# Moving the subtraction of the cumulative sums, 256 instructions, from VectorE to GpSimd in a Mamba-2 and ternary-FFN kernel

## The chip, the cores and the metric

The kernel runs on one core of a Trainium2 chip. A core has a matrix engine (TensorE, PE in the profile), three engines for elementwise work (VectorE or DVE, ScalarE or ACT, GpSimd or POOL) and a queue that issues the DMAs (SyncE, SP). Each engine takes its instructions in the order in which the program lists them and waits on semaphores for the others. The metric is device time in microseconds, lower is better.

## The reference

4096 tokens (2 sequences of 2048, width 512) go through a Mamba-2 layer, a residual sum and layer norm, a gated feed-forward layer with ternary weights, and a second residual sum and layer norm, all in float32. What matters here is the scan of the Mamba layer:

```python
dA = jnp.moveaxis(dtr * A, -1, -2)
xdt = xr * dtr[..., None]
Lmat = _segsum_exp(dA)      # exp(cum[s] - cum[z]) for z <= s, else 0
Y_diag = jnp.einsum('bcshn,bczhn,bchsz,bczhp->bcshp', Ch, Bh, Lmat, xdt)
cum = jnp.cumsum(dA, axis=-1)
decay_states = jnp.exp(cum[..., -1:] - cum)
states = jnp.einsum('bczhn,bchz,bczhp->bchpn', Bh, decay_states, xdt)
...
Y_off = jnp.einsum('bcshn,bchpn,bchs->bcshp', Ch, prev_states, jnp.exp(cum))
y = (Y_diag + Y_off).reshape(b, l, h, p)
...
hidden = silu(x @ wu.T) * (x @ wg.T);  out = hidden @ wd.T
```

There are 8 heads of 128 channels and a state of 64. The reference's chunks have 64 tokens; the kernel uses chunks of 128, which gives the same sums. For each chunk and head it needs the differences cum[s] - cum[z] for all 128x128 pairs of tokens. Only those with z <= s count, and for these the difference is at most zero; the kernel limits the others to zero so that the exponential cannot overflow, and masks them later.

## The kernel before

**Tiling.** The tokens are taken in 16 groups of 256 (`TG`), each of two chunks of 128 (`NC`). `proj(g)` does the input projections of a group, `steps(g)` the step sizes and the cumulative sums, `exps(g)` the exponentials, and `scan(g, c)` the scan of a chunk with the output projection. After that the feed-forward layer runs in 8 blocks of 512 tokens (`pair`, `down`); each of its products is made of seven smaller ones in fp8 and fp16. The first 45 us of the profile are preparation, the groups lie at about 45 to 745 us, and the feed-forward layer fills the rest.

**The path of a group around the change.** `cmm` (line 860) is the matmul that makes the cumulative sums. VectorE copies them out of PSUM: `ct` (864), 16 rows of 128, and `cum` (865), one column for each chunk and head. SyncE writes `ct` to DRAM (867) and reads it back spread over all 128 partitions: `cr` (873), one tile of 128 partitions x 8 heads x 128 for each chunk, 512 KB, and `ec` (887), used for the part that comes from the state before. Then `seg` (878) subtracts from each 128x128 block of `cr` the column `cum` and limits the result to zero: 8 instructions for a chunk in two half-operations of four (`sg{c}{hf}`), 16 for a group, 256 in all. ScalarE takes the exponential of the whole tile in place: `xf` (896) for the first chunk, `xg` (897) for the second, and `xec` (899) for `ec`. These need another activation table than the SiLU work around them, so `xf` has been made to wait for the second chunk's `cr` and for both `ec` tiles too, to do all exponentials of a group in one visit to that table. In the scan `w` (919) takes one column of the exponential, `xw0` (934) weighs B with it for the matmul that makes the new state (`st`, 941), `m` (956, eight instructions) multiplies the tile by the step size and by B.C masked, `md` (958) adds the D term, and `yd` (963) multiplies the result with x. After that `yg` (965), the sum of squares `ssq` (970), `rs` (971), the power on GpSimd `pw` (972), `yh` (973), a DMA transpose `th` (974) and the output projection `o0` to `o2` (983) follow.

**The projections.** Each projection result in PSUM (`x0` to `x8`, line 779) goes through a convolution of four taps: the first on ScalarE (`t3`, 792), three on VectorE (794), then SiLU on ScalarE (`xs`, 798) and a transpose on PE (`xt`, 802), which ScalarE evicts (804). The gate columns (`z`, line 754) are evicted by ScalarE (768).

**GpSimd before.** Beside a few instructions at the start, GpSimd computes only powers of 128x1 columns: `pw` (972) in the scans, the same for the inputs (636) and in the layer norms (1206, 1254).

**What sets the order.** The program is recorded as a list of operations, each with an engine, an assumed cost and what it reads and writes. `Order.run` then makes the order of each engine: it walks through an assumed time, and of the operations that are ready for an engine takes the one with the smallest key. The keys are a table of numbers in the source (`KEYS`), one for each operation, which a search outside of the kernel has found; on the chip no key and no assumed cost is known, only the order that came out. Buffers are handed out in the same walk, so the order also decides which buffer an operation gets. The assumed cost of one `seg` instruction is 0.197 us on VectorE.

Of the kernel before, what the change touches and what calls it, by code (L numbers as in the profile page):

```python
# [23 lines left out]
NH = 8  # L24
# [17 lines left out]
140 139 245 183 268 349 233 268 348 194 134 321 296 448 210 232 291 190 119 151 181 177 348 247 218 261 115 305 164  # L42
156 191 164 299 171 402 237 384 367 385 734 917 930 182 172 214 387 415 409 155 325 203 200 94 160 411 337 214 337
306 163 337 337 398 327 152 395 396 161 424 399 370 532 576 542 630 514 661 622 639 762 564 135 134 239 197 239 175
264 316 219 65 355 279 384 295 420 283 449 508 614 674 694 896 928 938 689 786 668 873 896 964 889 1242 891 879 920
999 856 952 1038 862 772 996 138 22 76 34 102 42 112 114 329 138 130 112 99 188 298 84 176 176 107 -9 160 159 116
228 128 172 210 252 211 348 304 268 316 448 420 282 390 703 399 394 474 429 430 431 395 523 337 463 372 462 456 506
687 744 752 824 727 794 786 782 88 348 349 169 216 212 185 465 437 664 529 411 520 533 514 508 544 572 535 552 573
594 574 575 512 592 592 684 540 600 745 640 687 606 625 698 681 289 225 340 448 309 142 340 370 436 348 176 190 353
303 273 175 379 282 662 640 695 696 597 682 778 667 200 316 294 129 255 19 205 231 602 626 650 607 735 517 783 670  # L50
369 283 422 447 626 339 450 353 549 385 632 679 549 255 600 642 617 779 763 660 708 652 712 701 264 514 514 538 827
520 575 638 528 653 736 692 226 314 489 471 146 173 56 172 214 182 117 630 408 305 608 674 535 671 685 738 681 720
717 1085 685 717 932 870 877 900 873 849 862 891 839 950 947 1129 940 946 975 1019 997 898 913 1088 936 1171 1438
989 989 1139 1105 997 437 344 217 489 494 615 643 593 586 512 384 223 402 421 480 368 470 638 782 725 786 797 739
827 999 1068 421 391 426 397 406 450 807 777 511 453 602 559 538 638 675 710 1142 1095 1194 1098 1113 1034 1154 1228
940 1055 950 984 1020 1098 1229 1360 984 1048 1193 967 973 1187 1224 1086 531 551 671 557 576 776 937 1032 889 894
1312 1249 1199 1067 797 830 563 573 764 795 790 827 876 878 839 1007 748 903 912 1329 1056 1066 1158 1072 981 1141
998 1103 1170 1206 1444 1395 529 563 797 869 796 778 793 855 882 844 861 839 924 829 830 913 924 908 912 980 935 949
1046 1060 993 1059 1066 966 1272 193 389 496 575 873 572 615 680 629 1188 938 1028 916 1051 1133 1161 872 1133 1225
1078 1364 1222 1382 1412 1405 1415 1480 1388 1472 1405 1454 1474 1368 1476 1560 1475 1499 1564 1415 1338 1504 1438  # L60
1394 1526 1636 1374 1214 1537 1818 1314 767 595 684 789 809 880 893 748 1006 1054 796 718 816 838 802 984 1082 1249
979 789 988 1060 920 1363 1338 1294 701 655 707 599 719 875 1052 986 836 875 884 954 973 1184 1031 1013 1034 1078
1065 1107 1189 1229 1079 1122 1066 1215 1085 1215 857 1204 1355 1433 1172 1198 1018 1265 1347 1277 1356 1530 614 658
733 656 649 699 835 939 1324 1361 928 872 1286 1397 1030 1049 949 1047 1156 1374 1354 1024 1410 1321 1413 1070 1400
1305 1414 1269 1291 1285 1291 1295 1478 1156 1426 1215 1403 1303 1441 1446 1439 1769 1394 866 991 1300 1389 1379
1436 1406 1368 1637 1239 1522 1397 1289 1278 1546 1392 1528 1790 1537 1618 1612 1259 1635 1357 1711 1648 1599 1996
1848 1240 1288 1412 1359 1425 1235 1428 1557 1445 1443 1380 1334 1574 1479 1520 1614 1624 1640 1871 1749 1972 2068
1842 1771 1752 1797 1815 1863 1829 1704 1917 1920 1807 1989 1852 2037 1664 2336 1769 1954 1996 1986 1920 1827 1994
1818 1746 1933 1887 1822 869 1331 1482 1499 1511 1601 1522 1496 1478 1709 1313 1514 1516 1516 1491 1564 1435 1675
1495 1702 1559 1609 1538 1847 1635 1608 1536 1737 1709 1709 1623 1827 1750 1929 1552 1749 1700 1656 1692 1974 1869  # L70
1918 1759 1949 1877 1875 1983 1875 1701 1913 1402 1735 1613 1553 1580 1673 1541 1764 1317 1624 1590 1516 1496 1614
1510 1621 1455 1699 1581 1324 1524 1689 1665 1798 2011 1967 1689 1808 1909 1873 1660 1905 1251 1309 1632 1626 1716
1572 1437 1581 1772 1690 1692 1665 1740 1664 1697 1679 1789 1550 1792 1718 1811 1747 1919 2171 1754 1870 1861 2146
2078 1142 1229 1681 1732 1920 1867 1880 1546 2129 1933 1964 1802 1940 1784 1812 1705 1962 2095 2094 1878 1958 1936
2031 1906 1961 2109 2118 1986 2525 1816 1668 1775 1706 1694 1981 1786 1974 1838 2093 1857 1906 2115 1910 2020 1866
1984 2047 2155 1960 2107 1921 2179 2123 1998 2150 2055 2086 2121 2075 2026 2123 1953 2053 2077 1979 2079 2327 2178
2162 2282 2376 2291 2472 2482 2308 2258 2103 2339 2344 1886 1735 1754 1933 1963 1960 1829 1888 2162 2209 1782 2008
2008 2049 1977 2311 2168 2061 1973 2081 1936 1949 1795 2227 2141 2162 1805 1998 2012 1797 1874 2141 1970 2023 1830
1908 1695 1888 1973 2186 1990 1932 2122 2067 2181 2052 2123 1999 2130 2127 1685 2023 1776 1892 1799 1900 1884 2028
2122 2253 2334 2339 2329 2055 2330 2304 1960 2014 1954 1918 1998 2119 2112 1971 2099 1992 2257 2154 2144 2273 2191  # L80
2156 1483 1637 1927 2118 2183 2206 2115 2057 1942 2171 2120 2216 2359 2036 2147 2040 2086 2181 2341 2192 2259 2268
2310 2489 2266 2369 2526 2438 2489 1689 1833 2030 2182 2257 2240 2194 2247 2498 2251 2150 2213 2309 2141 2170 2164
2351 2370 2327 2539 2485 2355 2460 2421 2457 2462 2448 2606 2785 2328 2087 2227 2195 2202 2320 2285 2305 2421 2198
2239 2384 2272 2296 2412 2263 2332 2203 2645 2223 2450 2405 2616 2457 2539 2774 2490 2613 2502 2585 2673 2676 2732
2752 2541 2462 2657 2714 2693 2933 2749 2911 2908 2518 2768 2820 2995 2645 2771 2889 2355 2276 2340 2475 2361 2370
2531 2413 2605 2533 2411 2199 2395 2619 2460 2468 2543 2587 2264 2325 2494 2403 2293 2455 2375 2488 2610 2488 2604
2680 2552 2614 2716 3088 2659 2488 2624 2622 2570 2876 2729 2797 2398 2445 2620 2354 2452 2575 2626 2697 2374 2577
2420 2458 2490 2316 2674 2906 2869 2734 2332 2532 2477 2752 2583 2749 2664 2615 2632 2681 2642 2874 2764 2925 3149
3124 3048 3154 3124 3092 3076 2931 1999 2139 2305 2593 2611 2521 2384 2454 2587 2474 2539 2681 2547 2479 2616 2516
2465 2692 2555 2745 2690 2694 2678 2803 2696 2873 2817 2764 3052 2216 2399 2423 2687 2704 2561 2711 2688 2895 2630  # L90
2598 2527 2807 2618 2560 2590 2549 2890 2726 2957 3025 3119 2945 2875 2907 2947 2915 3215 3424 2205 2544 2494 2403
2242 2393 2370 2730 2358 2828 2878 2725 2800 2911 2557 2863 2467 2834 2956 2899 3018 2820 2684 2608 2702 2797 2723
2784 2875 2884 3020 2942 2983 2915 2994 2938 3056 3163 3100 3053 3057 3280 3118 3484 3444 3266 3320 3221 3341 3430
3163 3101 2969 3134 3139 3269 3211 3132 3262 3338 2760 2710 2599 2661 2539 2813 3129 3048 3083 3125 2898 2982 2836
3056 3043 3099 2978 3118 2762 2775 2693 3117 3110 3184 2756 2965 2546 2636 2733 3367 3087 3195 2698 2895 2586 2635
2631 3039 3099 3136 3164 3232 3074 3254 3142 3341 3190 3293 3103 3068 3288 3069 3062 3095 3132 3112 2518 2457 2752
2477 2558 2722 3017 2999 2682 3140 3249 3245 3217 3137 3071 3016 2785 2599 2669 2780 2747 3099 2615 3052 3037 2827
2860 3068 3101 2745 2769 3080 3044 3166 3125 3060 3222 3235 3300 3265 3337 3297 3324 3464 3418 2672 2432 3081 2834
2916 3185 3134 3233 3384 3161 3160 3284 3280 2867 3017 3196 3213 3407 3280 3289 3365 3338 3394 3319 3419 3437 3421
# [261 lines left out]
class Order:  # L361
# [48 lines left out]
    def keys(self):  # L410
        for o, k in zip(self.ops, KEYS.split(), strict=True):
            o.key = int(k) / 10
# [100 lines left out]
def mamba_ffn_kernel(  # L513
# [51 lines left out]
    with ExitStack() as ph:  # L565
# [266 lines left out]
        def steps(g):  # L832
# [36 lines left out]
            for c in range(NC):  # L869
# [5 lines left out]
                for hf in range(2):  # L875
                    def seg(c=c, cr=cr, hf=hf):
                        for h in range(hf * 4, hf * 4 + 4):
                            V.tensor_scalar(cr[:, h, :], cr[:, h, :], cum[:, c * NH + h:c * NH + h + 1], 0.0, ALU.subtract, ALU.min)  # L878
# [433 lines left out]
```

## Time and profile before

| | us |
|---|---|
| median of 3 runs (1355.98 to 1358.28) | 1356.5 |
| span of the profiled execution, first to last instruction | 1355.1 |
| PE busy | 1334.2 (98%) |
| VectorE busy | 1143.1 (84%) |
| ScalarE busy | 1041.0 (77%) |
| GpSimd busy | 80.4 (6%) |
| the 256 `seg` instructions on VectorE: busy, idle just before them | 54.0, 6.6 |

The median of the runs is 1.4 us above the span of the profiled execution, the fastest run 0.9 us. A matmul is busy in the profile from its start to the end of its way through the array, 0.27 us for one that follows the last after 0.11 us, so neighbours overlap and PE can be called busy over a short pause. GpSimd durations are rough.

### The profile page before, as it was taken

To read this page: it belongs to the slowest core of one execution; us is meant where nothing else is said; L and a number is where in the kernel's file an instruction comes from. 1 tells how busy PE (TensorE), PEld (TensorE's weight loads), DVE (VectorE), ACT (ScalarE), POOL (GpSimd) and SP (SyncE) were. 2 spreads that over 40 slices of the span, in tenths; PEclk is the share of its full clock that TensorE was granted. 3 is DMA by queue.
4 is the path that set the end of the run, shared out by engine and by line. 5 is a ranking of instruction groups with operands and counts; after the bars stand their busy time and mean duration, and the time that the engine had idled before them with its cause. 6 is when DMAs were issued, how large, how long until landed. Compare 5 with 4: busy or idle time off the path is not lost.

```text
span 1355.1 us, 28913 instructions
## 1 busy us (share of the span) xinstructions
PE 1334.2 (98%) x11024; PEld 1057.9 (78%) x11024; DVE 1143.1 (84%) x3070; ACT 1041.0 (77%) x1996; POOL 80.4 (6%) x127
## 2 busy tenths in 40 slices
PE   9999999999999999999999999999999999999997
PEld 7777667766776677777676788888888888888886
DVE  5988878878999889889888697987979797979985
ACT  8888777768788778787767695969778695959772
POOL 1000000000000010000000000101010100001000
PEclk9999999999999999999999999999999999999999
DMA  6445666534543553573439530413222231314101
GB/s 242 139 116 147 171 164 165 147 111 124 155 137 99 156 139 80 137 185 85 112 76 247 127 63 9 125 24 110 40 79 55 94 56 60 82 40 102 32 17 47
DMA packets 194811, 145.60 MB, mean 107 GB/s; under 512 B 140656, under 2 KB 151920, under 8 KB 194672
## 3 DMA queue, kind: packets, MB, share of 16 engines
q1 hardware_dynamic: 194672, 143.75, 40.7%
q8 instruction: 86, 1.41, 0.4%
q14 instruction: 53, 0.43, 0.1%
HBM read 89.84 MB, written 22.41 MB: 83 GB/s over the span
## 4 chain that ended last, share of the span: by engine, by line
PE 66%; DVE 17%; ACT 10%; DMA 4%; issue 2%; POOL 0%; SPq 0%; POOLq 0%; ACTq 0%; DVEq 0%
PE sd L1096 9%; PE mm L779 9%; PE po L983 8%; PE mm L754 8%; PE po L1148 5%; PE sd L1148 4%; PE mm L1096 3%; PE po L1096 3%; PE sd L963 3%; DVE acc L794 3%; PE ms L1148 2%; DVE cr L956 2%; PE ms L1096 2%; PE mm L1148 2%; PE tr L802 2%
## 5 line engine op out<-in xcount | busy, mean ns | idle before, releaser
L1096 PEld LDWEIGHTS <-wx 128*128 128x128 fp8e4 x2048 | 200.2, 98 | 27.3 <-issue 2.9
L794 DVE SCALAR_TENSOR_TENSOR acc<-mm,cwu,acc 128x256 f32<-128x256 f32 x405 | 189.3, 479 | 21.6 <-ACT acc L792 19.2
L779 PEld LDWEIGHTS <-wx 128*128 128x128 f16 x1620 | 155.6, 97 | 33.2 <-issue 1.1
L1096 PEld LDWEIGHTS <-wz 128*128 128x128 fp8e4 x1536 | 150.2, 98 | 22.8 <-issue 4.6
L779 PE MATMUL mm<-uh,wx 128*128 128x260 f16 x1080 | 142.8, 274 | 0.7 <-DVE acc L794 0.5
L754 PE MATMUL mm<-wz,uh 128*128 128x344 f16 x720 | 119.9, 309 | 2.5 <-DVE acc L794 1.4
L983 PE MATMUL po<-wo,th 128*128 128x512 f16 x512 | 121.0, 379 | 0.3 <-ACT js L986 0.3
L792 ACT ACTIVATE acc<-mm,cst,cwu 128x256 f32<-128x256 f32 x135 | 74.8, 556 | 33.3 <-PE mm L779 31.8
L754 PEld LDWEIGHTS <-uh 128*128 128x128 f16 x720 | 68.5, 98 | 37.5 <-issue 4.4
L983 PEld LDWEIGHTS <-th 128*128 128x128 f16 x512 | 49.0, 98 | 49.5 <-issue 1.2
L779 PE MATMUL mm<-ul,wx 128*128 128x260 f16 x540 | 82.1, 273 | 0.0
L768 ACT ACTIVATE sz<-mm,szs 128x344 f32<-128x344 f32 (+1 forms) x90 | 48.4, 539 | 33.1 <-PE mm L754 28.4
L956 DVE SCALAR_TENSOR_TENSOR cr<-cr,dt,gm 128x128 f32<-128x128 f32 x256 | 72.1, 347 | 0.3
L798 ACT ACTIVATE xc<-acc 128x256 f32<-128x256 f32 x128 | 52.3, 412 | 25.5 <-DVE acc L794 25.1
L754 PE MATMUL mm<-wz,ul 128*128 128x344 f16 x360 | 67.2, 309 | 0.0
L963 PE MATMUL sd<-xt,cr 128*128 128x128 f32 x512 | 66.5, 277 | 0.1
L963 PEld LDWEIGHTS sd<-xt,cr 128*128 128x128 f32 x512 | 62.0, 192 | 3.1 <-issue 0.7
L983 PE MATMUL po<-wo,tl 128*128 128x512 f16 x256 | 60.5, 379 | 0.0
L878 DVE TENSOR_SCALAR cr<-cr,cum 128x128 f32<-128x128 f32 x256 | 54.0, 281 | 6.6 <-DMA cr<-cum_scratch 6.6
L804 ACT ACTIVATE xt<-tr 128x256 f32<-128x256 f32 x128 | 47.9, 374 | 11.7 <-PE tr L802 10.7
L1148 PEld LDWEIGHTS <-xt 128*128 128x128 f16 x512 | 50.1, 98 | 6.6 <-DVE xt L1131 0.9
L802 PE MATMUL tr<-ident,xc 128*128 128x128 f32 x256 | 50.2, 278 | 0.2
(356 smaller groups left out, 3275.1 us busy)
## 6 DMA issues: line engine op xcount, KB each, us to landing
cr<-cum_scratch SPq DMA_DIRECT2D x32, 512.0 KB, 5.6
ec<-cum_scratch SPq DMA_DIRECT2D x64, 128.0 KB, 5.5
fraw<-in_wupT_dram SPq DMA_DIRECT2D x32, 256.0 KB, 3.4
s_scratch<-js SPq DMA_DIRECT2D x32, 256.0 KB, 2.3
x<-s_scratch SPq DMA_DIRECT2D x32, 256.0 KB, 3.1
fraw<-in_wgateT_dram SPq DMA_DIRECT2D x32, 256.0 KB, 3.1
fraw<-in_wdownT_dram SPq DMA_DIRECT2D x32, 256.0 KB, 3.1
uraw<-in_uT_dram SPq DMA_DIRECT2D x15, 520.0 KB, 3.8
```

Of the source, the lines that this page charges most:

```text
L754: T.matmul(ps[:, :ZC], (uh, ul)[a][:, k, HL + c * P:HL + (c + 1) * P], wz4[b]()[:, j, k, :], start=(n == 0), stop=(n == 11))
L779: T.matmul(ps[:, :TW], wx4[a]()[:, j, k, :], (uh, ul)[b][:, k, :], start=(n == 0), stop=(n == 11))
L792: op(f"t{j}3", "S", act(TG, 2), lambda: S.activation(acc.ap, ps[:, HL:TW], AF.Identity, bias=cb[:, j:j + 1], scale=tap(3)), r=[ps, kc] + k ...
L794: op(f"t{j}{k}", "V", stt(TG), lambda k=k: V.scalar_tensor_tensor(acc.ap, ps[:, 1 + k:1 + k + TG], tap(k), acc.ap, ALU.mult, ALU.add), r=[ ...
L798: op(f"xs{j}", "S", silu(TG), lambda: S.activation(xc.ap, acc.ap, AF.Silu), r=[acc], w=[xc], table="silu")
L802: T.transpose(tr[:, c * P:(c + 1) * P], xc[:, c * P:(c + 1) * P], ident)
L878: V.tensor_scalar(cr[:, h, :], cr[:, h, :], cum[:, c * NH + h:c * NH + h + 1], 0.0, ALU.subtract, ALU.min)
L956: V.scalar_tensor_tensor(cr[:, h, :], cr[:, h, :], dt[:, c, h:h + 1], gm.ap, ALU.mult, ALU.mult)
L963: T.matmul(yp[hf][:, i * P:(i + 1) * P], cr[:, h, :], xt[:, c, h, :], start=is_first(g, c), stop=(is_first(g, c) or i == 3))
L983: T.matmul(po.ap, t[:, k, :], wo3[b]()[:, k, :], start=(q == 0 and k == 0), stop=(q == 2 and k == 7))
L1096: T.matmul(bank_[:, fi * TG:(fi + 1) * TG], wt[:, kt, f * P:(f + 1) * P], xT[i][:, a, :, kt, :], start=(first and fi == 0 and n == 0), sto ...
L1148: T.matmul(bank_[:, s_ * TG:(s_ + 1) * TG], X[k][j][:, a, e, s_ * P:(s_ + 1) * P], wt[:, k, :], start=(first and s_ == 0 and k == 0 and a ...
```

## The change

The subtraction with its limit at zero is issued on GpSimd instead of VectorE, with the same tiles and the same values; nothing else in the computation changes. The assumed cost in the planner becomes 0.3 us for each instruction. The table of keys is replaced as a whole, with numbers ten times finer, so that the order of every engine, the DMA queue's included, is a new one from the beginning to the end.

```diff
 KEYS = """
-140 139 245 183 268 349 233 268 348 194 134 321 296 448 210 232 291 190 119 151 181 177 348 247 218 261 115 305 164
...
-13374 13478 13544 13584 13460 13428 13216 13539 13325 13239 13477 13532 13619 13275 13367 13487 13497 13434
...
+138470 110551 -118248 107267 -122697 103243 -6098 122038 32505 -74957 106546
 """
...
         for o, k in zip(self.ops, KEYS.split(), strict=True):
-            o.key = int(k) / 10
+            o.key = int(k) / 100
...
                     def seg(c=c, cr=cr, hf=hf):
                         for h in range(hf * 4, hf * 4 + 4):
-                            V.tensor_scalar(cr[:, h, :], cr[:, h, :], cum[:, c * NH + h:c * NH + h + 1], 0.0, ALU.subtract, ALU.min)
-                    op(f"sg{c}{hf}", "V", 4 * 0.197, seg, r=[cum], w=[(cr, hf)])
+                            G.tensor_scalar(cr[:, h, :], cr[:, h, :], cum[:, c * NH + h:c * NH + h + 1], 0.0, ALU.subtract, ALU.min)
+                    op(f"sg{c}{hf}", "G", 4 * 0.3, seg, r=[cum], w=[(cr, hf)])
```

The built programs differ in what they issue in two things: 256 instructions are on GpSimd instead of VectorE, and ScalarE has two more table loads. PE has the same matmuls and SyncE the same DMAs in another order. In the new GpSimd order the 16 subtractions of a group stand together or nearly so, the powers between and behind them.

## The prediction

> **What bounds the kernel now.** I read the page first (busy shares), then the chain that ended last, PE's waits in the scans (45 to 745 us), the groups of VectorE and GpSimd, and the timeline around single GpSimd instructions.
>
> ```profile
> PE 1334.2 (98%) x11024; PEld 1057.9 (78%) x11024; DVE 1143.1 (84%) x3070; ACT 1041.0 (77%) x1996; POOL 80.4 (6%) x127
> ...
> PE 66%; DVE 17%; ACT 10%; DMA 4%; issue 2%; POOL 0%; SPq 0%; POOLq 0%; ACTq 0%; DVEq 0%
> ```
>
> A busy PE need not be PE at its peak, so I looked at the chain in order of time for the step of one matmul:
>
> ```profile
> 467.14 1.75 PE mm L754 x12
> ...
> 477.32 2.68 PE mm L779 x24
> ...
> 753.10 2.62 PE sd L1096 x24
> ```
>
> That is 0.146, 0.112 and 0.109 us each, and the starts in the timeline keep these steps almost everywhere. PE is truly the bound. What is left to gain are its pauses, and in the scans they are few:
>
> ```profile
> PE mm L754 <- DVE acc L794: 1.4, 4, 0.5
> PE sd L1096 <- DMA uraw<-stg: 1.0, 1, 1.0
> PE ms L916 <- ACT BC L811: 0.7, 1, 0.7
> PE mm L754 <- ACT sz L768: 0.6, 1, 0.6
> PE mm L754 <- DVE v L766: 0.5, 1, 0.5
> PE mm L779 <- DVE acc L794: 0.5, 2, 0.3
> ```
>
> The windows of the scans hold 693.3 us of busy PE in 700, so 6.7 us idle; by the list of waits VectorE ended 3.4 us of that. The operation that moves is this one, and these are GpSimd's rows nearest to it:
>
> ```profile
> L878 DVE TENSOR_SCALAR cr<-cr,cum 128x128 f32<-128x128 f32 x256 | 54.0, 281 | 6.6 <-DMA cr<-cum_scratch 6.6
> ...
> L972 POOL TENSOR_TENSOR rs<-rs,mhalf 128x1 f32<-128x1 f32 x32 | 20.0, 625 | 457.7 <-DVE rs L971 374.6 <-DVE q L852 47.2 <-DVE ww L848 22.0
> ...
> masks.py:199 POOL TENSOR_SCALAR_AFFINE_SELECT ident<-ident 128x128 f32<-128x128 f32 x1 | 0.3, 292 | 0.1
> ...
> masks.py:197 POOL MEMSET ident<- 128x128 f32 x1 | 0.2, 204 | 0.3 <-POOLq L1302 0.3
> L1302 POOL MEMSET const-bfloat16-1.0<- 128x1 bf16 x1 | 0.1, 102 | 0.0
> ```
>
> **The change, part by part.** Sums are against the profiled span, 1355.1 us; the median of the runs is 1.4 us above it, and I add the difference to the median.
>
> *Taken from VectorE:* 256 instructions, 54.0 us busy and 6.6 us in which the whole in-order VectorE stood behind them for the `cr` DMA: 3.8 us of the 41.5 us that a group takes. None of it is on PE's path by itself; its worth is the PE pauses that VectorE ends. Bounds: 0 and 3.4 us. I take half, **-1.7 us**, because some of those pauses (`v`, the taps) come straight after a ScalarE step.
>
> *Price of one subtraction on GpSimd.* No row shows it. From below, the affine select of the same shape with one input: 0.292 us. From above, a power's 0.547 us (undisturbed in the timeline) plus 127 elements at the 0.80 ns that the memsets of 128x128 and 128x1 differ by: 0.65 us. It is nearest to the select, with a column operand more; on VectorE tiny instructions with a column operand take some 0.07 us longer (`szs` 0.219, `mv` 0.148). I take 0.36 us.
>
> *Waiting for VectorE.* The powers show that GpSimd is held up by some VectorE instructions. Undisturbed a power takes 0.547 us; this one started inside an addition of two SBUF tiles and ended 0.41 us after it:
>
> ```profile
> 168.65 0.69 DVE L958 TENSOR_TENSOR cr<-cr,dmat 128x512 f32<-128x512 f32 x1
> ...
> 168.82 0.93 POOL L972 TENSOR_TENSOR rs<-rs,mhalf 128x1 f32<-128x1 f32 x1 [1.76 <-DVE rs L971]
> ```
>
> Over the 47 powers in the scans the mean excess is 0.135 us (32 in the scans with a mean of 625 ns and 15 of the inputs with 804, against 547). So 0.50 us for each subtraction; the ends are 0.29 without a wait and 0.65 + 0.135 = 0.79. VectorE's rows with two SBUF inputs that lie in the scans (L956, L958, L975, L925, L934, L735, L1032 and the 16-column steps of `steps`), with L1026, under which powers were late too, sum to 306 us of the 665 us between the first and the last subtraction, 46%. The other direction is hardly seen: an `ec` product that began under a power took 0.697 us instead of 0.686, but a power reads one element and the subtraction 128. Bounds for VectorE: 0, and 256 x 0.46 x 0.36 = 42 us busy. That is less than the 60.6 us it gives up, so no term on the path.
>
> The Trainium skill says this as a rule (SBUF — State Buffer, "Who interferes with whom"): a VectorE instruction with two SBUF inputs and a GpSimd instruction that reads SBUF share a port under an exclusive lock, held for the whole instruction. It speaks against the change; the powers agree for GpSimd's side. By the rule VectorE would lose the 42 us and its relief shrink to 18 us; by the `ec` row it keeps nearly all 60. The skill also calls one-input work on GpSimd roughly line-rate (GPSIMD Engine Reference, "Engine selection"), which no row here shows for this operation; with its 1.03 cycles at 1.2 GHz an estimate is 0.11 us over the fixed part, near the select, and the sum would not move.
>
> *When the subtractions must be done.* In the trace a group's first `cr` tile lands 5.7 to 12.1 us after its `cmm` (median 8.4), the second 9.2 to 15.8 (median 11.5). VectorE was done 13.1 to 18.9 us after `cmm`. With a subtraction of D, GpSimd is done at 8.4 + 16 D, or 11.5 + 8 D if that is later: 13.8 us at 0.29, 16.4 at 0.50, 21.0 at 0.79. Against this stands ScalarE's arrival at `xf`. PE in order serves as a clock: I added the steps above along the new PE order, took PE's time of the last matmul whose eviction stands ahead of `xf` in ScalarE's order, and added 4.4 us, the median by which `xf` trailed it in the trace (3.5 to 6.1). For the 16 groups of the new order this gives 16.4, 18.4, 21.9, 16.5, 15.2, 24.5, 28.3, 19.4, 18.4, 31.9, 19.4, 16.1, 23.0, 22.5, 17.9, 17.1 us after `cmm`. At 0.50 two groups are late, by 1.5 us in all; at 0.29 none; at 0.79 ten, by 35 us. Behind a late `xf` queue the evictions and first taps on ScalarE that free PE's two projection banks; I take 1.5 us as covered by the banks. PE also waits directly: from the exponential to `st` it takes 1.06 + 0.16 + 0.69 us and handovers, some 2.5, and the new order has `st` 17.0 and 18.2 us after `cmm` in groups 3 and 0: late by 1.9 and 0.7 at 0.50. So **+2.5 us**; bounds 0, and 18 (half of 35, as a bank covers some of each wait).
>
> *Powers behind the subtractions.* GpSimd's queue is now shared: `pw` of a scan can stand behind 8 to 16 subtractions and behind the landing of `cr`, and behind it `yh`, the transposes and `o0`. The cover: `o0` is at least 10.0 us of PE work behind `yd` in the new order, and the rows between sum to 6.7 us (0.69, 1.05, 0.15, 0.55, 1.05, 3.2). Bounds 0 and 5 us (a wait of 4 us, 0.7 beyond the cover, in 7 of 32 scans); I take **+0.5**.
>
> *The new order itself.* PE has the same matmuls. SyncE's DMAs change order; `cr` and `ec` landings are taken as unchanged. ScalarE gets two table loads, 2 x 1.283 us, under its 23% idle: 0 (bounds 0 and 2.6). One thing can be read: how much PE work lies between a convolution's projection and its transpose. In the old order one of 128 such distances is below 4.5 us, in the new one 12, down to 3.1; the fastest way through (0.556 + 3 x 0.479 + 0.412 and handovers) took 2.96 us in the trace, the tenth fastest 3.5. Ten chains with about 0.3 us too little make **+3 us** (0 to 9). All else in the order is a new draw: 0, within -6 and +6.
>
> Sum: -1.7 + 2.5 + 0.5 + 3 = +4.3 us, span 1359.4, time 1356.5 + 4.3 = **1360.8 us**.
>
> **Rivals.**
> - *Faster: the freed VectorE lets the order close PE's pauses.* VectorE falls from 87% in the scans to about 79%; if all 6.7 us of PE's idle time there went, with subtractions near 0.3: 1350. For it: mean distances from projection to transpose are the same (15.2 and 14.8). Against it: PE has little left to give. It decides if a subtraction, waits included, stays below some 0.4 us.
> - *Much slower: the subtraction is dear.* At 0.65 us, or with GpSimd starved behind back-to-back VectorE instructions (one power at 578.59 us took 1.33 us under three additions), `xf` waits in ten groups: +18 - 1.7 + 3.5, about 1376. Against it: the select's 0.292.
> - *No change:* PE's queue absorbs all of it, 1354 to 1359. For it: the 98%.
> - *VectorE as the loser:* held by GpSimd's reads, the taps come late; 42 us busy back, but still below before: not above +5, 1362.
>
> **How the numbers follow.** A measurement tells about 0.2%, 2.7 us, from no change. Chances: the forecast, a loss of 3 to 10 us, 0.35; faster by more than 2.7 us, 0.27; no change 0.20; much slower 0.13; VectorE as the loser 0.05. Slower is 0.35 + 0.13 + 0.05 = 0.53. The range leaves out the upper half of the dear case and the lowest part of the faster one: 1347 to 1374. The likeliest case alone has 1359 to 1367.
>
> **What would show it.** Right: L878's group on GpSimd at 0.45 to 0.55 us with a spread, VectorE busy near 1100; some 2 us of ScalarE idle before `xf` ended by GpSimd, PE's pauses at transposes (L802) and `st` (L941) up by a few us, the rest of PE's steps unchanged. Wrong: a mean above 0.65, or PE idle in the scans below 5 us, or a change that sits in the feed-forward layer, where only the order differs.

## The result and the profile after

The changed kernel took 1412.1 us (median of 4 runs, 1411.1 to 1414.2), the kernel before 1357.4 us beside it: a ratio of 1.0403, interval 1.0388 to 1.0418. The forecast was 1360.8 us with a range up to 1374, so it had the sign and missed the size by 51 us.

The page of the changed kernel: the busy shares, the chain that ended last by engine, and the group of the subtraction. Lines of the changed kernel are those of before plus 62 (L878 is now L940, L972 is L1034, L896 is L958).

```profile
PE 1352.3 (96%) x11024; PEld 1064.5 (75%) x11024; DVE 1108.3 (78%) x2814; ACT 1044.3 (74%) x1998; POOL 273.3 (19%) x383
...
PE 60%; ACT 13%; DVE 11%; POOL 7%; DMA 5%; issue 3%; SPq 0%; POOLq 0%; ACTq 0%; DVEq 0%
...
L940 POOL TENSOR_SCALAR cr<-cr,cum 128x128 f32<-128x128 f32 x256 | 190.4, 763 | 90.1 <-DMA cr<-cum_scratch 71.1
```

The span of this execution is 1412.4 us. GpSimd is busy 19% of it, less than any other engine, and is yet 7% of the chain, where before it was 0%. The reason stands in the last row: one subtraction takes 763 ns on average, so the 16 of a group take some 12 us.

The durations of that line by the view of one line (minimum, median, maximum in ns):

```profile
L940 POOL TENSOR_SCALAR cr<-cr,cum x256: 705/714/1877, 61.0 to 783.6; 128x128 f32<-128x128 f32 x128
```

No subtraction took less than 705 ns. The median is almost the minimum, so the price is the instruction's own, and the few long ones add only 763 - 714 = 49 ns on average.

Who waited for GpSimd is found in ScalarE's waits (us in all, times, longest):

```profile
ACT yh L1035 <- POOL rs L1034: 22.9, 9, 6.1
ACT cr L958 <- POOL cr L940: 18.7, 7, 4.2
```

The first is `yh` waiting for a power, the second `xf` waiting for the subtractions. Before, the first was 2.6 us, and `xf` waited 0.5 us for the subtractions on VectorE. VectorE waits too: at `yl` for the late `yh` (9.5 us before), and at the step that takes the power of the inputs from GpSimd (1.1 us before):

```profile
DVE yl L1037 <- ACT yh L1035: 23.3, 11, 6.6
DVE sc L699 <- POOL iu L698: 6.3, 6, 4.3
```

ScalarE and VectorE are in order, so what they do for PE is late behind these waits, as PE's own waits show:

```profile
PE tr L864 <- ACT xt L866: 7.6, 4, 4.8
PE mm L841 <- DVE acc L856: 6.3, 5, 4.3
PE ms L696 <- ACT acc L854: 5.9, 1, 5.9
PE tr L864 <- ACT xc L860: 4.3, 2, 3.9
```

None of these rows names GpSimd. One stretch of the timeline shows the link (start, duration, instruction, idle time before it and what ended it), first GpSimd, then ScalarE, VectorE and PE:

```profile
329.53 13.33 POOL L940 TENSOR_SCALAR cr<-cr,cum 128x128 f32<-128x128 f32 x16 [1.10 <-DMA cr<-cum_scratch]
342.83 0.56 POOL L1034 TENSOR_TENSOR rs<-rs,mhalf 128x1 f32<-128x1 f32 x1
```

```profile
343.42 1.15 ACT L1035 ACTIVATE yh<-y,rs 128x1024 f16<-128x1024 f32 x1 [6.08 <-POOL rs L1034]
344.48 0.55 ACT L854 ACTIVATE acc<-mm,cst,cwu 128x256 f32<-128x256 f32 x1
...
345.89 0.19 ACT L794 ACTIVATION_READ_ACCUMULATOR uh<-uraw 128x1 f32 x1
```

```profile
344.61 1.28 DVE L1037 SCALAR_TENSOR_TENSOR yl<-y,rs,yh 128x1024 f16<-128x1024 f32 x1 [6.47 <-ACT yh L1035]
...
346.20 0.28 DVE L979 TENSOR_TENSOR gm<-ms,tri 128x128 f32<-128x128 f32 x1
```

```profile
338.82 1.90 PE L1045 MATMUL po<-wo,th 128*128 128x512 f16 x8
346.63 0.56 PE L696 MATMUL ms<-uss,ones 128*128 128x1 f32 x2 [5.91 <-ACT acc L854]
347.05 3.57 PE L1045 MATMUL po<-wo,th 128*128 128x512 f16 x8
```

Sixteen subtractions run for 13.3 us. The power of a scan, 0.56 us of work, stands behind them, and `yh` waits 6.1 us for it. PE's next instruction (L696) sums the squares of the next group's inputs over the partitions, which has nothing to do with that power. It needs `uss`, which ScalarE reads out at L794, in line behind `yh`; this is done at 346.08. And it needs the PSUM bank `ms`, from which VectorE's `gm` must first read. `gm` stands in line behind `yl`, which waits for `yh` too; it is done at 346.48. PE's weight load for L696 starts at 346.60. The view names the tap (L854), but L696 neither reads nor writes what the tap uses; `gm` came last.

The last row holds a second loss. The eight matmuls of `po` take 1.90 us ahead of the pause and 3.57 us behind it. The granted clock of PE, the sixth figure after the length of each window here (busy time of PE, PEld, DVE, ACT and POOL come first), was half in between:

```profile
335.00:345.20 10.20, 5.72 (x40) 3.62 (x37) 2.16 (x5) 4.12 (x8) 8.39 (x13) 1.00 0.35 95
345.30:352.00 6.70, 5.37 (x18) 2.74 (x19) 5.19 (x14) 4.43 (x8) 0.68 (x1) 0.50 0.02 5
353.00:360.00 7.00, 6.65 (x55) 4.67 (x54) 4.18 (x14) 5.73 (x8) 0.00 (x0) 1.00 0.74 194
```

The trace of the changed kernel has seven such stretches at 0.5 before its last microseconds, 34.1 us in all; each begins within 1.7 us of the end (before or after it) of a PE pause of 2.4 us or more, though one pause of 2.75 us has none. The kernel before has none, the new order without subtractions one of 3.4 us.

### The profile page after: what moved, and what is told of

The parts are those of the page before. It is cut to its first block, busy times and chain, and to the rows that moved or that the text cites. A ratio compares the mean times of both kernels' runs of the same rounds, so it can differ in the third digit from the quotient of the medians.

```text
span 1412.4 us, 28987 instructions
## 1 busy us (share of the span) xinstructions
PE 1352.3 (96%) x11024; PEld 1064.5 (75%) x11024; DVE 1108.3 (78%) x2814; ACT 1044.3 (74%) x1998; POOL 273.3 (19%) x383
## 4 chain that ended last, share of the span: by engine, by line
PE 60%; ACT 13%; DVE 11%; POOL 7%; DMA 5%; issue 3%; SPq 0%; POOLq 0%; ACTq 0%; DVEq 0%
PE sd L1158 10%; PE sd L1210 7%; PE mm L841 7%; POOL cr L940 7%; PE po L1045 7%; PE mm L816 6%; PE po L1158 4%; PE mm L1158 4%; DMA cr<-cum_scratch 3%; DVE acc L856 2%; PE sd L1025 2%; PE po L1210 2%; PE ms L1158 2%; PE mm L1210 2%; PE ms L1210 1%
## 5 line engine op out<-in xcount | busy, mean ns | idle before, releaser
L940 POOL TENSOR_SCALAR cr<-cr,cum 128x128 f32<-128x128 f32 x256 | 190.4, 763 | 90.1 <-DMA cr<-cum_scratch 71.1
L1158 PEld LDWEIGHTS <-wz 128*128 128x128 fp8e4 x1536 | 150.2, 98 | 22.9 <-issue 4.1
L1045 PE MATMUL po<-wo,th 128*128 128x512 f16 x512 | 125.5, 389 | 5.1 <-DMA th<-yh 3.0
L1316 POOL TENSOR_TENSOR lnr<-lnr,mhalf 128x1 f32<-128x1 f32 x32 | 21.9, 688 | 438.1 <-DVE lnr L1253 416.1
L854 ACT ACTIVATE acc<-mm,cst,cwu 128x256 f32<-128x256 f32 x135 | 75.1, 558 | 28.4 <-PE mm L841 26.6
L1034 POOL TENSOR_TENSOR rs<-rs,mhalf 128x1 f32<-128x1 f32 x32 | 19.5, 609 | 270.9 <-DVE rs L1033 203.9
L860 ACT ACTIVATE xc<-acc 128x256 f32<-128x256 f32 x128 | 52.5, 413 | 20.0 <-DVE acc L856 17.3
```

Of the source, the lines that this page charges most:

```text
L854: op(f"t{j}3", "S", act(TG, 2), lambda: S.activation(acc.ap, ps[:, HL:TW], AF.Identity, bias=cb[:, j:j + 1], scale=tap(3)), r=[ps, kc] + k ...
L860: op(f"xs{j}", "S", silu(TG), lambda: S.activation(xc.ap, acc.ap, AF.Silu), r=[acc], w=[xc], table="silu")
L940: G.tensor_scalar(cr[:, h, :], cr[:, h, :], cum[:, c * NH + h:c * NH + h + 1], 0.0, ALU.subtract, ALU.min)
L1045: T.matmul(po.ap, t[:, k, :], wo3[b]()[:, k, :], start=(q == 0 and k == 0), stop=(q == 2 and k == 7))
L1158: T.matmul(bank_[:, fi * TG:(fi + 1) * TG], wt[:, kt, f * P:(f + 1) * P], xT[i][:, a, :, kt, :], start=(first and fi == 0 and n == 0), sto ...
```

## The experiments

**The rest without the subtraction.** The new order is kept, the subtractions are left out.

```diff
-                        for h in range(hf * 4, hf * 4 + 4):
+                        for h in range(hf * 4, hf * 4):
```

> The new order with the 256 subtractions left out (cr is not shifted nor limited before the exponential; all else as in the changed kernel). Theory A (the price of a subtraction on GpSimd, 0.76 us with its waits instead of the 0.50 I assumed, makes exponentials and powers late; the order itself is sound): the loss of 55 us goes almost wholly, 1348 to 1360 us. Theory B (the new order itself is bad on this chip, for instance by its short distances from projection to transpose): at most a third of the loss goes, 1394 us or more.

It took 1367.7 us, 1.0077 (1.0060 to 1.0094). That lies between the two ranges, nearer the first. So of the 55 us, 44.4 belong to the subtractions on GpSimd and some 11 to the new order without them. The waits of ScalarE for GpSimd are almost back to before:

```profile
ACT yh L1035 <- POOL rs L1034: 3.3, 4, 2.2
```

**The order of before without the subtraction.**

```diff
-                        for h in range(hf * 4, hf * 4 + 4):
+                        for h in range(hf * 4, hf * 4):
```

> The kernel before with the 256 subtractions left out on VectorE, in the old order. It prices VectorE's relief and nothing else. By the prediction's term: 1.7 us less than before, bounds 0 and 3.4, so some 1355 us. If the new order without subtractions (1367.7 us) is to be compared like with like, it is this run that stands beside it: the order is then worse by the difference, 12 to 13 us. A rival, that the old order gains much more from an empty VectorE (10 us or more), would make the new order worse still.

It took 1356.7 us, 0.9996 (0.9987 to 1.0005). Taking the work off VectorE altogether, without putting it anywhere, is worth 0.6 us, which can't be told from nothing. The new order's own price is therefore 1367.7 - 1356.7 = 11.0 us.

**Half and three quarters of the subtractions**, in the new order.

```diff
-                        for h in range(hf * 4, hf * 4 + 4):
+                        for h in range(hf * 4, hf * 4 + 2):
```

> The new order with two of the four subtractions in each half-operation left out: GpSimd needs some 5.7 us for a group instead of 11.4 to 12.2, as if one subtraction took 0.36 to 0.38 us. It is the case that the prediction was worked out for. Theory A: the formula of the prediction holds for that price, 1355 to 1364 us. A rival within A, that the price enters steadily and not above a threshold: half of the loss, about 1385 us. Theory B: 1394 us or more.

```diff
-                        for h in range(hf * 4, hf * 4 + 4):
+                        for h in range(hf * 4, hf * 4 + 3):
```

> The new order with one of the four subtractions in each half-operation left out: 12 x 0.714 = 8.6 us for a group, as if one subtraction took 0.54 us. It tests the prediction's threshold at the price that it had assumed (0.50). From the landings and the exponentials of the run without subtractions, four groups are late, by 2.4 us in all, and the powers wait up to 8.6 us: by the threshold 1370 to 1378 us. A price that enters steadily over the whole range (11 us at 0, 55 at four of four) would give about 1401 us.

Half took 1368.8 us, 1.0089 (1.0074 to 1.0104), hardly more than none; three quarters 1381.5 us, 1.0176 (1.0160 to 1.0191). They lie 4.8 and 3.5 us above the ranges expected; the first range left out what the new order costs by itself. Of ScalarE's waits, first with half, then with three quarters:

```profile
ACT yh L1035 <- POOL rs L1034: 5.2, 7, 2.2
```

```profile
ACT yh L1035 <- POOL rs L1034: 12.3, 8, 3.6
ACT cr L958 <- POOL cr L940: 2.5, 4, 1.1
```

So the loss is no constant for each instruction. A group has room for some 6 us of GpSimd work (6.1 us with half); what exceeds it shows up as waits for GpSimd, and as time.

**Only the exponentials late.** The powers of the scans and of the inputs are replaced by VectorE instructions that write constants, so that no power stands behind the subtractions (the normalisation of the scan's output and the scale of the inputs are left out).

```diff
-            op(nm + "pw", "G", 0.6, lambda: G.tensor_tensor(inv(), sc.ap, half[:, 0:1], ALU.pow), r=[sc, *r], w=[key])
+            op(nm + "pw", "G", 0.6, lambda: V.tensor_scalar(inv(), sc.ap, 0.0, 0.0445, ALU.mult, ALU.add) if nm == "us" else G.tensor_tensor(inv(), sc.ap, half[:, 0:1], ALU.pow), r=[sc, *r], w=[key])
...
-            o("pw", "G", 0.6, lambda: G.tensor_tensor(rs[:, 1:2], rs[:, 0:1], mhalf[:, 0:1], ALU.pow), w=[rs])
+            o("pw", "G", 0.6, lambda: V.tensor_scalar(rs[:, 1:2], rs[:, 0:1], 0.0, 512.0, ALU.mult, ALU.add), w=[rs])
```

> The changed kernel with the powers of the scans and of the inputs taken off GpSimd: VectorE writes a constant in their place (the normalisation of the scan's output and the scale of the inputs are left out). The subtractions stay on GpSimd, which has nothing else in the scans. If the late exponentials alone carry the loss (ScalarE waited 18.7 us for the subtractions at xf): 1400 to 1412 us. If the powers queued behind the subtractions carry a good part (ScalarE waited 22.9 us for them at yh): 1375 to 1395 us. Theory B: no change.

It took 1391.4 us, 1.0256 (1.0240 to 1.0271): 23.7 us above the order without subtractions. ScalarE's only wait for GpSimd is now

```profile
ACT cr L958 <- POOL cr L940: 21.6, 8, 3.9
```

**Only the powers late.** GpSimd does 16 subtractions for a group at the same time as before, but on a tile of its own that nobody reads; one 128x1 instruction for each chunk waits for the landing of `cr`. The exponentials take the tile as it landed (`cr` isn't shifted).

```diff
+                        h = hf * 4
+                        if not seen:
+                            seen.append(1)
+                            G.tensor_scalar(dummy[:, :1], cr[:, h, :1], cum[:, c * NH + h:c * NH + h + 1], 0.0, ALU.subtract, ALU.min)
...
-                            G.tensor_scalar(cr[:, h, :], cr[:, h, :], cum[:, c * NH + h:c * NH + h + 1], 0.0, ALU.subtract, ALU.min)
+                            G.tensor_scalar(dummy, dummy, cum[:, c * NH + h:c * NH + h + 1], 0.0, ALU.subtract, ALU.min)
```

> The new order with the subtractions done by GpSimd on a tile of its own, behind one 128x1 instruction for each chunk that waits for the landing of cr: GpSimd is busy as long as in the changed kernel, the powers queue behind it, but no exponential waits for a full tile (cr is not shifted before the exponential). It separates the powers from the exponentials. If the two add up (removing the powers took 20.7 us off): 1368 + 21, 1383 to 1395 us. If the powers' wait counts only because the exponentials before it are late too: 1368 to 1378 us. If the powers carry more than their share, as both waits lie on ScalarE and overlap: above 1398 us.

It took 1409.1 us, 1.0379 (1.0364 to 1.0394): 41.4 us above the order without subtractions.

```profile
ACT yh L1042 <- POOL rs L1041: 34.9, 10, 8.0
```

Late powers alone cost nearly all of it, late exponentials alone half. Together that is 65 us and not 44.4. It fits that both waits lie on ScalarE, so that where it is held at `xf`, it comes to `yh` later and waits less there (22.9 us in the changed kernel against 34.9); no run separates this from the longer GpSimd work of this run. Side by side, with the time over the order without subtractions. PE's pauses are the idle time just before its instructions, summed over the trace; the stretches at half clock leave out the one at each kernel's end:

| | GpSimd, us a group | ScalarE waits for GpSimd at `yh`, `xf` | VectorE waits for the inputs' power | PE's pauses | PE at clock 0.5 | time, us | over the first row |
|---|---|---|---|---|---|---|---|
| no subtractions | 0 | 3.3, 0 | 1.9 | 19.4 | 3.4 | 1367.7 | 0 |
| half | 6.1 | 5.2, 0 | 3.5 | 20.3 | 0 | 1368.8 | 1.2 |
| three quarters | 9.1 | 12.3, 2.5 | 4.3 | 29.8 | 10.2 | 1381.5 | 13.8 |
| exponentials late only | 12.0 | 0, 21.6 | 0 | 36.3 | 20.5 | 1391.4 | 23.7 |
| powers late only | 13.5 | 34.9, 0 | 6.9 | 46.4 | 44.4 | 1409.1 | 41.4 |
| the changed kernel | 11.9 | 22.9, 18.7 | 6.3 | 51.9 | 34.1 | 1412.1 | 44.4 |

(The GpSimd column is the busy time of the subtractions divided by the 16 groups. With late powers only it includes the 11.9 us, over all groups, of the small instructions; without these it is 12.7, so that run has somewhat more GpSimd work in front of the powers than the changed kernel, and its 41.4 us is an upper value of their part. The powers of the inputs are among those late in it.)

From the third row on, PE's pauses grow by 0.7 to 1.0 us for each microsecond that ScalarE and VectorE wait more for GpSimd: in the last row 51.9 - 19.4 = 32.5 against 38.3 + 4.4 = 42.7. Most of the rest of the time is PE at half clock behind the pauses. Each matmul step in these stretches, compared with the usual step of the same shapes, adds up to 16.2 us in the changed kernel against 1.7 in the first row, 14.5 more. The two come to 47 us where the spans differ by 45; the other steps vary by as much.

Of the pauses of more than 1 us in the changed kernel's groups, 35.5 us in all, 17.3 lead back to GpSimd through ScalarE's queue alone, 5.9 through ScalarE's and VectorE's (the stretch above), 4.3 through VectorE waiting for the power of the inputs, and 1.3 through the exponential that `st` needs; the rest does not lead back to it so directly.

**The price by form.** Thirty-two GpSimd instructions behind the last power of the kernel before, where VectorE does almost nothing; only their durations count here, as the instructions also lengthen the end of the kernel (its time was 1382.2 us).

```diff
+            d2, c1 = dmat.rearrange("p h s -> p (h s)"), cst[:, 0:1]
+            for n in (1, 128, 256, 512):
+                for i in range(4):
+                    G.tensor_scalar(d2[:, :n], d2[:, :n], c1, 0.0, ALU.subtract, ALU.min)
+            for i in range(4):
+                G.tensor_scalar(d2[:, :P], d2[:, :P], c1, None, ALU.subtract)
+            for i in range(4):
+                G.tensor_scalar(d2[:, :P], d2[:, :P], 0.5, 0.0, ALU.subtract, ALU.min)
+            for i in range(4):
+                G.tensor_scalar(d2[:, :P], d2[:, :P], 0.5, None, ALU.subtract)
+            for i in range(4):
+                G.tensor_tensor(d2[:, :P], d2[:, :P], ident, ALU.subtract)
```

> The kernel before with 32 GpSimd instructions behind its last power, on a tile that is no longer used; results are unchanged, the time is longer by their sum. They price the subtraction by its parts, with VectorE almost idle: column operand and two operations at widths 1, 128, 256 and 512; one operation; immediate operands; and a two-tile subtraction. If the fixed part is dear, the width hardly matters: width 1 near 0.55 us, as the power's. If it is the price of an element, width 1 lies near 0.25 us and 512 near 2.2 us. If the column operand or the second operation makes it dear, the forms without them lie near the select's 0.29 us.

The groups by form (after the bar: busy us and mean ns of one). L1271 is the kernel's form at four widths; then come two operations with constants (L1275), one with the column (L1273), one with a constant (L1277), and the subtraction of two tiles (L1279).

```profile
L1271 POOL TENSOR_SCALAR dmat<-dmat,cst 128x512 f32<-128x512 f32 x4 | 8.0, 1995 | 0.4
L1271 POOL TENSOR_SCALAR dmat<-dmat,cst 128x256 f32<-128x256 f32 x4 | 4.6, 1142 | 0.4
L1271 POOL TENSOR_SCALAR dmat<-dmat,cst 128x128 f32<-128x128 f32 x4 | 2.9, 729 | 0.4
L1275 POOL TENSOR_SCALAR dmat<-dmat 128x128 f32<-128x128 f32 x4 | 2.6, 640 | 0.3
L1273 POOL TENSOR_SCALAR dmat<-dmat,cst 128x128 f32<-128x128 f32 x4 | 2.4, 607 | 0.4
L1277 POOL TENSOR_SCALAR dmat<-dmat 128x128 f32<-128x128 f32 x4 | 2.1, 531 | 0.3
L1279 POOL TENSOR_TENSOR dmat<-dmat,ident 128x128 f32<-128x128 f32 x4 | 1.8, 454 | 0.3
L1271 POOL TENSOR_SCALAR dmat<-dmat,cst 128x1 f32<-128x1 f32 x4 | 1.3, 324 | 0.3
```

From 256 to 512 columns the instruction grows by 853 ns, 3.33 ns for each column of 128 elements, on about 0.29 us by these two widths (0.324 us was measured at one column). The column in place of a constant adds 0.08 to 0.09 us and the second operation about 0.11 to 0.12; the rest, 0.53 us, is the plain one-input instruction.

**The new order with the subtraction on VectorE.**

```diff
-                            G.tensor_scalar(cr[:, h, :], cr[:, h, :], cum[:, c * NH + h:c * NH + h + 1], 0.0, ALU.subtract, ALU.min)
+                            V.tensor_scalar(cr[:, h, :], cr[:, h, :], cum[:, c * NH + h:c * NH + h + 1], 0.0, ALU.subtract, ALU.min)
```

> The new order with the subtractions issued on VectorE at the places in the program where GpSimd had them; the whole computation is kept. Theory A: VectorE does a group in about 3.2 to 4.5 us, exponentials are in time, but VectorE carries 54 us that the order did not plan there: 1355 to 1370 us. Theory B: 1394 us or more.

It took 1379.2 us, 1.0168 (1.0151 to 1.0185), above the range expected and 11.5 us above the same order without them; in the order of before the same instructions at VectorE are worth 0.6 us. PE waits for VectorE at the taps, which the order of before has at 1.4 us and 0.5:

```profile
PE mm L816 <- DVE acc L856: 6.1, 6, 2.7
PE mm L841 <- DVE acc L856: 3.8, 7, 1.4
```

So the new order seems to rely on VectorE being free at the places where the subtractions now stand on its queue.

**Half on each engine**, heads taken in turn, in the new order.

```diff
-                            G.tensor_scalar(cr[:, h, :], cr[:, h, :], cum[:, c * NH + h:c * NH + h + 1], 0.0, ALU.subtract, ALU.min)
+                            (G, V)[h % 2].tensor_scalar(cr[:, h, :], cr[:, h, :], cum[:, c * NH + h:c * NH + h + 1], 0.0, ALU.subtract, ALU.min)
```

> The new order, whole computation, with the heads of each half-operation given in turn to GpSimd and VectorE: 128 subtractions on each. GpSimd needs about 5.7 us for a group, as in the run with half of them left out. Threshold theory (only subtractions that outlast ScalarE's way to the exponential, or the powers' due time, cost anything): 1368 to 1374 us, that is the new order's own 1367.7 and a little for VectorE's 27 us. If the price enters steadily, or VectorE and GpSimd hold each other up when they read the same tile in turn: 1385 us or more.

It took 1373.8 us, 1.0120 (1.0105 to 1.0134), in the range expected of a threshold. It is the best of the versions here that do the whole computation in the new order, and still behind the kernel before. It has both engines on the same work in one execution:

```profile
L940 POOL TENSOR_SCALAR cr<-cr,cum x128: 707/716/1838, 60.9 to 743.5; 128x128 f32<-128x128 f32 x128
```

```profile
L940 DVE TENSOR_SCALAR cr<-cr,cum x128: 270/286/429, 61.8 to 742.1; 128x128 f32<-128x128 f32 x128
```

**The keys of before, with GpSimd and a true price in the plan.**

```diff
-                            V.tensor_scalar(cr[:, h, :], cr[:, h, :], cum[:, c * NH + h:c * NH + h + 1], 0.0, ALU.subtract, ALU.min)
-                    op(f"sg{c}{hf}", "V", 4 * 0.197, seg, r=[cum], w=[(cr, hf)])
+                            G.tensor_scalar(cr[:, h, :], cr[:, h, :], cum[:, c * NH + h:c * NH + h + 1], 0.0, ALU.subtract, ALU.min)
+                    op(f"sg{c}{hf}", "G", 4 * 0.71, seg, r=[cum], w=[(cr, hf)])
```

> The subtractions on GpSimd, with the keys of the kernel before and an assumed cost of 0.71 us in the walk that makes the order, so that the order is made for the true price but not searched for it. If the wrong assumed cost is what made the change dear: 1360 to 1385 us. If a chain through GpSimd of 11.4 us for a group costs much in any order that these operations allow: above 1395 us.

It took 1432.1 us, 1.0551 (1.0536 to 1.0565), more than the changed kernel, although ScalarE now waits much less for GpSimd:

```profile
ACT yh L973 <- POOL rs L972: 7.5, 10, 1.7
ACT cr L896 <- POOL cr L878: 1.0, 2, 0.7
```

The true price in the plan did move the subtractions out of ScalarE's way, and every other operation with them, by keys that were found for another plan: PE's pauses sum to 64.8 us against 13.2 before, also in the feed-forward layer (25.7 against 5.4), where no subtraction is. The run fits that a wrong assumed cost made the crowding at GpSimd, but it has other keys too, so it does not show it; mending the cost without a new search did not pay.

**Two halves for the transposes.** My reading of the new order's own loss was that transposes come too soon after their projection. To tell whether they wait for the SiLU output or for the PSUM bank to be free, they alternate between two halves of the bank, in the new order without subtractions and in the kernel before.

```diff
+                        turns.append(0)
+                        hv.append(len(turns) % 2 * TG)
...
-                            T.transpose(tr[:, c * P:(c + 1) * P], xc[:, c * P:(c + 1) * P], ident)
+                            T.transpose(tr[:, hv[0] + c * P:hv[0] + (c + 1) * P], xc[:, c * P:(c + 1) * P], ident)
...
```

> The new order without subtractions, with the transposes of the projections (L864 in the changed kernel) written in turn to the two halves of their PSUM bank, so that a transpose need not wait for the eviction of the one before. It looks into the 11 us that the new order loses by itself, of which 3.8 us are PE's longer waits at these transposes and 1.8 at that of B. If the waits are for the bank: 1362 to 1365 us. If they are for the SiLU output that comes too late, as the prediction had it (projections too close ahead of their transposes): 1366 to 1368 us.

> The kernel before with the same two halves for the transposes; whole computation. PE's waits at the transposes in the old order are 0.8 us in all: 1355.5 to 1357.5 us, not to be told from before. It is here as the only version at hand that might beat both.

They took 1369.0 us, 1.0083 (1.0069 to 1.0097), where 1367.7 had been without the edit, and 1356.9 us, 0.9996 (0.9987 to 1.0004). The first is just above both of its ranges, so nothing was gained. But that does not clear the bank, as the waits did not go. First without the two halves, then with them (where the lines are two further on):

```profile
PE tr L877 <- ACT xt L866: 1.5, 2, 0.9
PE tr L864 <- ACT xt L866: 1.4, 2, 0.9
PE tr L864 <- ACT xc L860: 0.4, 1, 0.4
PE tr L864 <- ACT bt L879: 0.3, 1, 0.3
```

```profile
PE tr L879 <- ACT xt L868: 2.4, 2, 1.5
PE tr L866 <- ACT xt L868: 1.4, 2, 0.9
```

`xt` is the eviction of the transpose before, `xc` the SiLU output, and the transpose of B (L877, then L879) was not moved. One such wait in the run with two halves:

```profile
65.97 0.42 ACT L860 ACTIVATE xc<-acc 128x256 f32<-128x256 f32 x1
...
70.94 0.37 ACT L868 ACTIVATE xt<-tr 128x256 f32<-128x256 f32 x1
```

```profile
71.36 0.44 PE L866 MATMUL tr<-ident,xc 128*128 128x128 f32 x2 [0.92 <-ACT xt L868]
```

The SiLU output had been ready since 66.4 us, and PE started when the other half had been evicted. So in this program the transpose still waits for the eviction, whichever half it writes, and what a free bank would be worth stays open. By its pauses, PE stands 6.2 us longer in the new order without subtractions than before: 3.7 at the transposes, 2.2 at `o0` and 1.6 at the projections of x, with less at the gate columns and 0.2 less in the feed-forward layer. One stretch at half clock adds 1.7 us. The rest of the 11 us is spread over steps that are a little longer; what makes it is left open.

## Why the prediction was wrong, point by point

**What bounds the kernel:** right, but not complete. PE is busy 96% after, and most of the loss is in its pauses: 13.2 us before, 19.4 in the new order without subtractions, 51.9 in the changed kernel. That its steps keep their length did not hold: behind long pauses they doubled, at a granted clock of 0.5, which is some 14.5 of the further 44.4 us. The sum had no term for it.

**Taken from VectorE, -1.7:** it was 0.6 (0 within its interval), inside the bounds of 0 and 3.4. The chain had put 17% on VectorE before; that share was not a gain to be had.

**The price of a subtraction, 0.36 us with ends at 0.292 and 0.65:** this failed; it took 0.714, outside both ends. The fixed part of the upper end, a power's 0.547 us, was too high (0.324 us at one column), which hid part of the error. The failing step is the 0.80 ns for an element, taken from two memsets: a memset only writes, and with an input, a column and two operations it is 3.33 ns. The affine select as nearest row was wrong in the same way, since it too took 0.292 for all its 128 columns. The text had named a mean above 0.65 as the sign that it was wrong.

The Trainium skill calls one-input work on GpSimd roughly line-rate (GPSIMD Engine Reference, "Engine selection"). The runs disagree for this instruction: 3.33 ns for a column, against an estimate of 0.86 ns from the 1.03 cycles at 1.2 GHz of the same page, and 714 ns in all where VectorE took 281. The measurement decides.

**Waiting for VectorE, 0.135 us, and VectorE's loss, 0 to 42 us:** the first was 0.05, mis-sized on the other side, so that by luck the whole, 0.763, came to lie within the 0.29 to 0.79 given for it, at the upper end. What was wrong in it is the 46%: the VectorE rows that it counted ran beside the subtractions for 29 of their 190 us, 15%. That VectorE would not be the loser was right: all its other instructions together took 1301.5 - 1295.0 = 6.5 us more than before (1108.3 busy is not their sum, as neighbours overlap).

The skill's rule of a port held exclusively for a whole instruction (SBUF — State Buffer, "Who interferes with whom") agrees with the long subtractions: the 30 that ran beside a VectorE instruction with two SBUF inputs for more than 0.3 us have 11.7 of the 14.8 us by which all 256 exceed 705 ns. The 42 us on VectorE's side did not come, as the two met so much less.

**When the subtractions must be done, +2.5 (0 to 18):** PE's order as a clock was right, its use wrong. In the new order without subtractions `xf` started, after `cmm`, at 15.4, 17.7, 21.6, 16.0, 17.2, 24.0, 29.0, 19.5, 21.5, 31.5, 21.6, 16.3, 23.2, 21.8, 17.7 and 16.2 us; 13 of the 16 estimates are within 1.0 us. With 0.763 in place of 0.50 the same table has ten groups late by 31 us; the run with only the exponentials late measured eight by 21.6. The landings, taken as unchanged, came later in the new order without subtractions: the first `cr` tile by 1.0 us and the second by 2.1 (medians). The step that failed, beside the price, is "half of 35, as a bank covers some of each wait", and "covered by the banks" for the 1.5: with only the exponentials late, a wait of 21.6 us became 16.9 us more of PE's pauses, not half of it, and with 8.5 us of steps at half clock it cost 23.7.

The group at 61 us shows why. GpSimd, then ScalarE, then PE:

```profile
61.03 11.22 POOL L940 TENSOR_SCALAR cr<-cr,cum 128x128 f32<-128x128 f32 x16 [22.28 <-DMA cr<-cum_scratch]
```

```profile
72.28 1.06 ACT L958 ACTIVATE cr<-cr 128x1024 f32<-128x1024 f32 x1 [3.94 <-POOL cr L940]
```

```profile
75.58 0.69 PE L864 MATMUL tr<-ident,xc 128*128 128x128 f32 x2 [4.85 <-ACT xt L866]
```

ScalarE waits 3.9 us, PE 4.9, and not at a bank of the projections but at a transpose, for which ScalarE had to evict the one before (`xt`) behind the exponential. I had looked at one kind of work behind `xf` and priced its cover; the queue holds several, and here one without cover decided.

**Powers behind the subtractions, +0.5 (0 to 5):** this is the term that failed most. Alone it is up to 41.4 us. The cover that I worked out, 10.0 us of PE work before `o0` against 6.7 us of rows, held for what it was about: the list of PE's waits has 3.0 us at `o0` for `th`, and 2.3 without subtractions. But I followed the result of `yh` only to `o0`. I left out the instructions behind `yh` on ScalarE, which stand still with it, those behind `yl` on VectorE (23.3 us of waiting for `yh`, 8.0 without subtractions), and the powers of the inputs, which stand behind the subtractions as well (VectorE waited 6.3 us, PE once 4.3). The wait was taken too small as well: 4 us in 7 scans were assumed, 9 waits of up to 6.1 came. My question about an added wait, what is queued behind the waiting instruction, I had asked for `xf` and not for `yh`.

**The new order itself, +3 and 0 within 6:** 11.0 in all, inside the 15 that the two upper bounds make together, but far from the 3 taken. The transposes came near the 3 us (3.7 us of pauses), but by luck: the term stood for a SiLU output that comes too late, and of PE's waits there only 0.4 us are for it, 3.2 for the eviction of the transpose before. "All else in the order" came to the remaining 7 instead of 0, beyond the end of its range. That the order was made for an assumed 0.3 us shows in GpSimd's time for a group, 4.8 us in the plan and 11.1 to 13.7 on the chip.

**The rivals.** The dear subtraction was the right one, with the wrong end: 1376 at 0.65, because it too carried half the waits at `xf` and only 0.5 us for the powers. (Its ten groups and 18 us belong to 0.79; at 0.65 the same table has eight groups late by 14 us.) The gain by a freed VectorE fell with the 0.6 us, and its stated condition, a subtraction below some 0.4 us, wasn't met. Where all subtractions are left out, which is the best that it could hope for, the order of before has 1356.7.

## What to carry to other kernels

When an instruction on an in-order engine comes to wait, follow the queue behind it, and the queue behind each reader of its result: here each microsecond that ScalarE and VectorE waited more for GpSimd became 0.7 to 1.0 us of PE's pauses, though the path to `o0` was covered. Where the pauses are long, look at the granted clock behind them and count the longer steps too. An engine that is busy 6% of the time is not free if short steps of other chains pass through it; what counted here was how long a block was put in front of them (6.1 us a group was nearly free, 9.1 was not). And a duration for a new operation should not be built from rows of instructions that do less for each element: measure it first, or take the worst.

## What was not expected of the hardware

- GpSimd's subtraction of two tiles, 454 ns for 128x128, is faster than the subtraction of a constant from one tile, 531, and of a column, 607.
- GpSimd took 3.33 ns for each column of 128 elements with one input, a column operand and two operations, over a fixed 0.29 us; VectorE does the same 128x128 instruction in 281 ns.
- Behind a long pause PE ran at a granted clock of 0.5 for 3.4 or 6.8 us (up to 10.2 us in the run with only the powers late), and its steps took about twice as long: eight matmuls of 128x512 took 3.57 us instead of 1.90. In the changed kernel that is some 16 us, about a third on top of the pauses themselves.
